# A hybrid of a two-way scan, convolution and attention: sums moved between engines, one image buffer halved, and a new set of due times

## Chip, cores and metric

The kernel runs on one core of a Trainium2 chip. The metric is the device time of one execution in microseconds; several executions are timed and their median is given. The core has five engines, each with its own instruction queue that is worked off in order: TensorE (PE, with its weight loads as PEld), VectorE (DVE), ScalarE (ACT), GpSimd (POOL) and SyncE (SP), which here only issues the transfers. All transfers of the main loop go through SP's one queue.

## The reference, cut

Eight images of 384 channels and 32 x 32 positions go through two layers.

```python
# layer 0, for each image
xn = rmsnorm(x)                                  # over channels
# mamba, forward and on the reversed tokens:
u, z   = split(xn @ in_proj.T)
u      = silu(conv1d(u))                         # 4 taps along tokens
dt, Bm, Cm = split(u @ x_proj.T)                 # 24, 16, 16
delta  = softplus(dt @ dt_proj.T + b)
h      = exp(delta * A) * h + (delta * u) * Bm   # 384 channels x 16 states, token by token
y      = sum_n(h * Cm) + u * D
y      = (y * silu(z)) @ out_proj.T
g      = (forward + backward) * scale_mod
local  = sigmoid(conv3x3(xn) + b) * xn
x      = x + res_scale * (g + local)
# layer 1, on tokens t (1024 x 384)
t = t + causal_attention(layernorm(t))
t = t + gelu(layernorm(t) @ kron(c_fc_1, c_fc_2).T) @ kron(c_proj_1, c_proj_2).T
```

The feed-forward's first weight is a Kronecker product of a 1536 x 32 and a 1 x 12 matrix. So layernorm(t) @ w_fc.T is a weighted sum over 12 neighbouring channels (weights c_fc_2, called c2 in the kernel), which leaves 32 numbers per token, followed by a product with c_fc_1.

## The kernel before

The kernel is in float32. It records all its instructions first, with a due time for each, and then a planner (`Plan`) puts them in order: it holds a cost for every instruction, lets each engine take the instruction that is ready by those costs and has the lowest rank (due time less a rush), gives out the buffers, and issues the whole list in that order. What runs on the chip is thus a fixed order on each queue, with semaphores in between. All instructions that are recorded so are put down to the helper's line L423, so the profile's groups are told apart by the names of tiles.

The time axis of the due times is counted in units of the scan. For each image there are four steps (`STEPS`): direction 1 on the second half of the tokens, direction 1 on the first half, direction 0 on the first, direction 0 on the second; a half has 512 tokens. In this text they are steps 0 to 3. Each step has 12 units (k = 0 to 11), so an image has 48. One unit of `scan` handles 64 channels with 8 of the 16 states, on 128 partitions (16 channels x 8 states) by 4 x 512:

- GpSimd multiplies du (delta times u, loaded as hs<-db) with B (br) in one instruction of 128 x 2048: hs<-hs,br.
- ScalarE makes four times exp(delta A) into PSUM (da<-dl,nega), in three buffers da.
- VectorE runs four scans along the tokens (hs<-da,hs).
- The product with C is one instruction of 128 x 2048. In units 2, 5, 8 and 10 (`POOL_C`; 1, 3, 6, 8 and 10 in the last image, `POOL_END`) it runs on GpSimd (hs<-hs,cr), in the others on VectorE (hs<-hs,cb).
- TensorE sums over the states into y (y<-hs,sel), which frees the buffer hs, of which there are five.

Everything else is spread over these units by due times. For an image b, `norm_in` (normalizing, the in-projection of u, and the store of the normalized image xn to the scratch xq, padded for the 3 x 3 convolution), `conv_tokens` and `prepare` (delta, B and C) run in the units of image b - 1 (`OTHERS`; image 0 has `FIRST`, image 1 `SECOND`). `local_branch` (the gate z, the 3 x 3 convolution and the local branch) runs at the end of the units of image b - 1. `project` (the out-projection, after steps 2 and 3), `attention` and `feed_forward` for each half (`LAYER1`) run from the last steps of the image itself into the units of the next one. Counted in units, the feed-forward of the first half falls into step 0 of the next image, that of the second half into step 2; the local branch falls into step 3 and the beginning of the next step 0.

Places that the change touches:

- xn (one buffer) holds a whole image of 3 x 32 x 33 per partition from `norm_in` until the second half's local branch has been computed.
- `local` loads x again into a tmp, multiplies the gate with xn and adds x, both on GpSimd (uc<-uc,xn and tmp<-tmp,uc), and stores the sum to the scratch lx.
- `project` loads lx as three tmp and lets TensorE transpose them into the same PSUM bank as the out-projection (w<-ident,tmp).
- `feed_forward` multiplies each normalized tile of tokens with c2 on GpSimd (xt<-xt,row_sb), sums 12 neighbours on VectorE (xr<-xt), and turns the sums with four matmuls of 32 columns per tile (w<-ident,xr).
- tmp has five buffers.

While nothing else is ready, the planner puts a matmul with zeros into y's open bank (y<-zero,ident), called a filler here.

Of the kernel before, what the change touches and what calls it, by code (L numbers as in the profile page):

```python
# [28 lines left out]
AX = mybir.AxisListType  # L29

P = 128
HB = 512
STEPS = [(1, 1), (1, 0), (0, 0), (0, 1)]
POOL_C = (2, 5, 8, 10)
POOL_END = (1, 3, 6, 8, 10)
TMP, SIDE = 5, 4
REPS = 4
RUSH = 3.54
START, LATER = -40.0, -8.0
LATER_US = 36.0  # L40


FIRST = (1, 3.32, 9.89, 13.26, 18.58, 22.35)
SECOND = (23.0, 0.55)
OTHERS = (4.41, 7.19, 11.9, 15.22, 22.12, 25.54, 30.53, 33, 41.81, 48.93)
BURST = 8.0
PROJECT = 1.79
LAYER1 = (39.24, 51.32, 61.95, 72.21, 83.03)
LAYER1_6 = (40.39, 50, 56.13, 65.96, 72.89)
LAYER1_7 = (37.95, 41.37, 46.15, 55.8, 61.15, 67.54, 71.0, 75.0, 81.0)  # L50
HASTE = 19.01
FREE = ["w", "da", "cb", "w", "da", "cb", "da"]
EXPS = 0.0
SCAN = (-1.34, -1.1, -0.6, -0.4, -0.33, 0.15, 0.75, 1.2)
class _Op:


# [19 lines left out]
class Plan:  # L77
# [8 lines left out]
    SWITCH = 1.3  # L86
    LOOSE = ("w", "tmp", "side")
    HURRY = 6.54
    PATIENCE = 1.92
    SETTLE = 0.2  # L90
    HOP = 0.18
    RATE = 300e3
    LAND = 2.54
    GATE = 3.413
    WARM, COLD = 0.8, 0.45
    KEEP = 0.65
# [330 lines left out]
def conv_attn_kernel(  # L427
# [21 lines left out]
    NB, C, H, W = x.shape  # L449
    L = H * W  # L450
    NC = C // P
# [3 lines left out]
    NJ = cp1T.shape[1]  # L455
    NI = C // NJ
    NF = cp1T.shape[0] // P
    NG = P // NJ
# [3 lines left out]
    NQ = 4  # L462
# [39 lines left out]
    def weight(shape, nm):  # L502
        return plan.tile(const, shape, nm)
# [199 lines left out]
        cp2.unsqueeze(1).to_broadcast([P, NJ, NI]),  # L703
    )
    emat = emat.rearrange("p j i -> p (j i)")
    plan.tile(ps_y, [P, HB], "y")
    plan.nothing = plan.slots["y"][0][:, :256], ident, zero.to_broadcast([P, 256])
    carry = weight([P, NU * SG, NQ], "carry")
# [5 lines left out]
    def tmp():  # L714
        return plan.tile(l0, [P, HB], "tmp", TMP)

    def load_x(b, h):
# [3 lines left out]
            plan.sync.dma_start(xt[cc], xv[b, :, cc, h * HB : (h + 1) * HB])  # L721
        return xt

    def xn_of(b, h):

        return xn_t[b][:, :, h * HR : (h + 1) * HR, :W]

    def norm_in(b, h):
        xt = load_x(b, h)
        yield  # L730
        if b not in xn_t:
            xn_t[b] = plan.tile(l0, [P, NC, H, WP], "xn")
        xn = xn_of(b, h)
# [13 lines left out]
        padded = xn_t[b][:, :, h * HR : (h + 1) * HR]  # L747
        plan.vector.memset(padded[:, :, :, W:], 0.0)
        at = 1 + (h * HR + 1) * WP
        for cc in range(NC):  # L750
            plan.sync.dma_start(
                xq[cc * P : (cc + 1) * P, at : at + HR * WP],
                padded[:, cc].rearrange("p r w -> p (r w)"),
            )
        yield
        for m in range(NC):
            pu = bank()
            for cc in range(NC):
                plan.tensor.matmul(
                    pu.rearrange("p (r w) -> p r w", w=W),  # L760
                    win[:, cc, m * P : (m + 1) * P], xn[:, cc],
                    start=cc == 0, stop=cc == NC - 1,
                )
            u = tmp()
            plan.scalar.copy(u, pu)
            plan.sync.dma_start(up[m * P : (m + 1) * P, UP + h * HB : UP + (h + 1) * HB], u)
            yield
# [31 lines left out]

    def local(b, h):  # L800

        cols = slice(h * HB, (h + 1) * HB)
        lx = lx_t[b, h] = plan.tile(dram, [C, HB], "lx", 4)
        sg = sg_t[b, h]
        sgf = sg.rearrange("p cc t -> p (cc t)")
        plan.scalar.activation(sgf, sgf, AF.Identity, bias=hrs, scale=hrs)
        for cc in range(NC):
            xt = tmp()
            plan.sync.dma_start(xt, xv[b, :, cc, cols])
            sgi = sg[:, cc].rearrange("p (r w) -> p r w", w=W)  # L810
            plan.gpsimd.tensor_mul(sgi, sgi, xn_of(b, h)[:, cc])
            plan.gpsimd.tensor_add(xt, xt, sg[:, cc])
            plan.sync.dma_start(lx[cc * P : (cc + 1) * P], xt)
            yield

    def gate(b, h):
# [131 lines left out]
    def scan(b, si, lo=0, hi=HB):  # L948
# [38 lines left out]
        for k in range(n_u):  # L987
# [93 lines left out]
    def project(b, h, t1, lo=0, hi=HB):  # L1081

        yz = [yz_t[b, h, lo, cc] for cc in range(NC)]
        lx = []
        for cc in range(NC):
            lx.append(tmp()[:, : hi - lo])
            plan.sync.dma_start(lx[cc], lx_t[b, h][cc * P : (cc + 1) * P, lo:hi])
        yield
        for i in range((hi - lo) // P):
            cols = slice(i * P, (i + 1) * P)  # L1090
            po = bank()
            for cc in range(NC):
# [4 lines left out]
            for cc in range(NC):  # L1097
# [22 lines left out]
    def normed(t1, ti0, nrm, i):  # L1120
        xt = plan.tile(l1, [P, C], "xt", 2)
        plan.scalar.activation(
            xt, t1[:, ti0 + i], AF.Identity,
            scale=nrm[:, 0, i : i + 1], bias=nrm[:, 1, i : i + 1],
        )
        return xt

    kv_t = {}

    def attention(b, t1, t0, n, end=False):  # L1130
# [7 lines left out]
        tile0, nt = t0 // P, n // P  # L1138
        nrm = token_norm(t1, tile0, nt)
        yield  # L1140
        if end:
            xT = plan.tile(l0, [P, NQ * HB], "hs", 5)[:, : NC * n]
            xT = xT.rearrange("p (cc t) -> p cc t", cc=NC)
        else:
            xT = plan.tile(l1, [P, NF // 2, HB], "gl")[:, :NC, :n]
        for i in range(nt):
            xt = normed(t1, tile0, nrm, i)
            pt = bank()
            for cc in range(NC):
                plan.tensor.transpose(  # L1150
                    pt[:, cc * P : (cc + 1) * P], xt[:, cc * P : (cc + 1) * P], ident
                )
            plan.scalar.copy(
                xT[:, :, i * P : (i + 1) * P],
                pt[:, :C].rearrange("p (cc t) -> p cc t", cc=NC),
            )
            yield

        cs = tmp()[:, :n]
# [87 lines left out]
    def feed_forward(b, t1, t0, n, direct=False):  # L1247
# [1 line left out]
        nrm = token_norm(t1, tile0, nt)  # L1249
        yield  # L1250

        xr = plan.tile(l1, [P, NT, NJ], "xr")
        for i in range(nt):
            xt = normed(t1, tile0, nrm, i).rearrange("p (j i) -> p j i", i=NI)
            plan.gpsimd.tensor_mul(xt, xt, c2.unsqueeze(1).to_broadcast([P, NJ, NI]))
            plan.vector.reduce_sum(xr[:, i], xt, axis=AX.X)
            yield
        px = bank()[:, :n]
        for i in range(nt):
            for g in range(NG):  # L1260
                plan.tensor.matmul(
                    px[g * NJ : (g + 1) * NJ, i * P : (i + 1) * P], xr[:, i], ident,
                    start=True, stop=True, skip_group_check=True,
                )
        xrT = plan.tile(l1, [P, HB], "q")[:, :n]
        plan.scalar.copy(xrT, px)
        yield
# [57 lines left out]
        plan.batch = None  # L1325

    def local_branch(b, h, a, e):
        plan.spread(gate(b, h), a, a + 0.4 * (e - a))
# [145 lines left out]
```

## Time and profile before

| | |
|---|---|
| Runs | 3231.9, 3232.3, 3235.58, 3239.41 us |
| Median of these | 3233.94 us |
| Profiled execution | 3253.27 us |
| Its span, first to last instruction | 3251.5 us |
| Mean granted clock of TensorE | 0.96 of full speed |
| DMA | 762.47 MB, mean 235 GB/s |
| Busy share of the DMA engines, early (120 to 400 us) | 0.93 to 0.94 |
| Busy share of the DMA engines, middle (400 to 790 us) | 0.82 |
| After the last scan (3133 to 3251.5 us) | 118.5 us: PE 108.5 busy, ACT 67.2, DVE 44.1, POOL 15.2 |

How to read what follows: a group's row gives the engine, the operation, output <- inputs by tile names, shapes and count, then busy time and the mean of one in ns, then the idle time of the engine just before these instructions and what ended it. A row of the stretches gives a piece of the span, its length, and the busy time of each engine in it. A row of the waits gives who waited for whom: total us, how often, and the longest. Matmuls in float32 appear as two rows in the trace for each one that is built, transposes as one.

### The profile page before, as it was taken

The page shows a single profiled execution, that of the slowest core. Times are in us where ns is not written, and L with a number is a line of the kernel's source. Part 1 is how long each engine was busy: PE and PEld are TensorE (multiplying, and loading weights), DVE is VectorE, ACT ScalarE, POOL GpSimd, SP SyncE. Part 2 cuts the span into 40 slices and gives each one's busy share as a digit, 9 for nine tenths or more (in the row PEclk, how much of TensorE's full clock was granted, in tenths as well). Part 3 has the DMA queues.
Part 4 walks back from the last instruction along what each step waited for, and adds up shares of the span by engine and source line. Part 5 has one row for each costly group of instructions (what it writes and reads, how often), then busy time and mean ns, then how long its engine had stood idle before and what let it go on. Part 6 is the DMA issues. An engine that isn't in the chain of part 4 may idle for free. (4 is left out here: it accounts for less than half of the span.)

```text
span 3251.5 us, 40064 instructions
## 1 busy us (share of the span) xinstructions
PE 2791.4 (86%) x11945; PEld 1189.7 (37%) x11945; DVE 2679.0 (82%) x2740; ACT 2216.5 (68%) x3609; POOL 2693.4 (83%) x923
## 2 busy tenths in 40 slices
PE   8887888988888888888789888898888888888789
PEld 3322333343333333343333433333333333333345
DVE  3688778797898798987999878988899879989972
ACT  3565566768676775868678676777767686677564
POOL 2888889788998889897898989888898878998950
PEclk8988999999999999999999999999999999899899
DMA  7999998778887797977978789787878779665520
GB/s 226 273 289 270 274 270 261 239 227 251 257 250 245 232 268 214 288 231 219 279 240 271 221 256 255 232 270 233 259 230 261 223 230 278 196 193 180 178 87 23
DMA packets 424462, 762.47 MB, mean 235 GB/s; under 512 B 51020, under 2 KB 70804, under 8 KB 424244
## 3 DMA queue, kind: packets, MB, share of 16 engines
q1 hardware_dynamic: 424116, 759.80, 77.7%
q8 instruction: 94, 1.54, 0.2%
q14 instruction: 124, 1.02, 0.1%
q0 software_dynamic: 128, 0.11, 0.0%
HBM read 617.92 MB, written 141.80 MB: 234 GB/s over the span
## 5 line engine op out<-in xcount | busy, mean ns | idle before, releaser
L423 POOL TENSOR_TENSOR hs<-hs,br 128x2048 f32<-128x2048 f32 (+1 forms) x395 | 1738.6, 4407 | 313.0 <-PE y L423 139.1
L423 ACT ACTIVATE da<-dl,nega 128x512 f32<-128x512 f32 (+1 forms) x1584 | 1055.6, 677 | 539.1 <-DVE hs L423 383.3
L423 DVE TENSOR_TENSOR_SCAN hs<-da,carry,hs 128x512 f32<-128x512 f32 (+1 forms) x816 | 938.9, 1202 | 150.4 <-ACT da L423 126.4
L423 DVE TENSOR_TENSOR_SCAN hs<-da,hs 128x512 f32<-128x512 f32 x768 | 883.5, 1202 | 147.4 <-ACT da L423 127.2
L423 POOL TENSOR_TENSOR hs<-hs,cr 128x2048 f32<-128x2048 f32 (+1 forms) x137 | 599.0, 4372 | 77.9 <-DVE hs L423 44.7
L423 DVE TENSOR_TENSOR hs<-hs,cb 128x2048 f32<-128x2048 f32 (+1 forms) x259 | 574.5, 2218 | 62.9 <-ACT carry L423 52.3
L423 PE MATMUL y<-hs,sel 128*32 128x512 f32 (+1 forms) x3168 | 481.4, 613 | 134.4 <-POOL hs L423 85.5
L423 PE MATMUL y<-zero,ident 128*128 128x256 f32 x1394 | 369.9, 397 | 0.0
L423 PEld LDWEIGHTS y<-zero,ident 128*128 128x128 f32 x1394 | 257.5, 196 | 147.7 <-issue 120.0
L423 PEld LDWEIGHTS y<-hs,sel 128*32 128x32 f32 x3168 | 89.9, 110 | 386.4 <-POOL hs L423 140.0
L421 ACT ACT_TABLE_LOAD x178 | 228.4, 1283 | 3.1
L423 PE MATMUL w<-q,fc1s 128*128 128x512 f32 (+1 forms) x388 | 195.3, 612 | 18.1 <-ACT gl L423 7.1
L423 PE MATMUL w<-v,p 128*128 128x384 f32 x546 | 197.2, 507 | 14.4 <-ACT p L423 12.9
L423 PE MATMUL w<-rep,cwt 128*32 128x512 f32 x744 | 180.0, 626 | 32.7 <-DMA rep<-up 27.1
L423 PE MATMUL w<-rep,cit 96*32 96x512 f32 x1152 | 176.8, 627 | 24.3 <-DMA rep<-xq 12.6
L423 PE MATMUL w<-wout,side 128*128 128x384 f32 x378 | 147.6, 521 | 36.7 <-DVE side L423 29.3
L423 ACT ACTIVATE uc<-w,vec 128x512 f32<-128x512 f32 x144 | 97.0, 679 | 92.5 <-PE w L423 76.1
L423 ACT COPY gl<-w 128x512 f32<-128x512 f32 (+2 forms) x254 | 136.9, 549 | 32.4 <-PE w L423 31.1
L423 PE MATMUL w<-xn,wz 128*128 128x512 f32 x288 | 138.1, 621 | 7.3 <-ACT uc L423 4.9
L423 PE MATMUL w<-xn,win 128*128 128x512 f32 x288 | 135.3, 611 | 4.7 <-ACT tmp L423 2.7
L423 PE MATMUL w<-wvs,gl 128*128 128x384 f32 x372 | 133.7, 501 | 5.5 <-ACT v L423 3.2
L423 PEld LDWEIGHTS w<-v,p 128*128 128x128 f32 x546 | 102.0, 195 | 99.3 <-ACT p L423 33.3
(204 smaller groups left out, 3201.6 us busy)
## 6 DMA issues: line engine op xcount, KB each, us to landing
dl<-dd SPq DMA_DIRECT2D x744, 256.0 KB, 5.7
hs<-db SPq DMA_DIRECT2D x744, 256.0 KB, 5.8
rep<-up SPq DMA_DIRECT2D x180, 257.5 KB, 6.1
rep<-xq SPq DMA_DIRECT2D x192, 222.4 KB, 6.3
tmp<-in_x_dram SPq DMA_DIRECT2D x96, 256.0 KB, 6.1
dd<-tmp SPq DMA_DIRECT2D x96, 256.0 KB, 4.6
db<-uc SPq DMA_DIRECT2D x96, 256.0 KB, 4.6
br<-bd SPq DMA_DIRECT2D x62, 256.0 KB, 4.8
```

Of the source, the lines that this page charges most:

```text
L421: self.nc.scalar.preload_act_table_set(table)
L423: op.call(*args, **{k: self._bind(v) for k, v in op.kw.items()})
```

## The change

- *Feed-forward's first sum.* The product with c2 on GpSimd, the sum on VectorE and the 16 small matmuls of a half are gone. Each tile of normalized tokens is transposed by TensorE (three transposes), evicted by ScalarE, and three matmuls with a matrix cmat (made once, c2 spread over channels and repeated for the four groups) give the sums for the half.
- *Adding x.* `local` no longer loads or adds x and stores the product with xn alone to lx. `project` loads three more tmp with x and transposes them into the same bank: six transposes per tile of 128 tokens in place of three.
- *The image by halves.* xn holds a half (3 x 16 x 33). `norm_in` stores it to xq as before; `local_branch` first loads the half back from xq (`load_xn`), due one unit before the branch.
- *tmp* has seven buffers in place of five.
- *Products with C.* In steps 0 and 2 five units (1, 4, 6, 8, 10) run them on GpSimd, in steps 1 and 3 four (2, 5, 8, 10), as before. The last image keeps its own set.
- *Due times and planner costs.* `FIRST`, `SECOND`, `OTHERS`, `LAYER1` and its variants, `SCAN`, `RUSH`, `HASTE`, and the planner's `PATIENCE`, `SETTLE`, `HOP` and `LAND` get other numbers, so that the whole order changes.

```diff
-POOL_C = (2, 5, 8, 10)
+POOL_C = ((1, 4, 6, 8, 10), (2, 5, 8, 10), (1, 4, 6, 8, 10), (2, 5, 8, 10))
-TMP, SIDE = 5, 4
+TMP, SIDE = 7, 4
-RUSH = 3.54
+RUSH = 2.75
-FIRST = (1, 3.32, 9.89, 13.26, 18.58, 22.35)
-SECOND = (23.0, 0.55)
-OTHERS = (4.41, 7.19, 11.9, 15.22, 22.12, 25.54, 30.53, 33, 41.81, 48.93)
+FIRST = (1, 3.88, 11.84, 15.58, 19.14, 21.28)
+SECOND = (21.3, 0.613)
+OTHERS = (4.45, 7.23, 12.19, 15.26, 22.16, 25.58, 30.33, 33.04, 41.85, 48.97)
-LAYER1 = (39.24, 51.32, 61.95, 72.21, 83.03)
+LAYER1 = (39.19, 52.83, 61.9, 73.47, 83.81)
-HASTE = 19.01
+HASTE = 27.94
-SCAN = (-1.34, -1.1, -0.6, -0.4, -0.33, 0.15, 0.75, 1.2)
+SCAN = (-1.34, -1.14, -0.48, -0.4, -0.33, 0.15, 0.75, 1.2)
...
-    PATIENCE = 1.92
-    SETTLE = 0.2
-    HOP = 0.18
+    PATIENCE = 1.86
+    SETTLE = 0.28
+    HOP = 0.0
-    LAND = 2.54
+    LAND = 2.73
...
+    def load_xn(b, h):
+        xn_t[b, h] = half_image()
+        for cc, rows in enumerate(rows_of(b, h)):
+            plan.sync.dma_start(xn_t[b, h][:, cc].rearrange("p r w -> p (r w)"), rows)
...
     def local(b, h):
...
         for cc in range(NC):
-            xt = tmp()
-            plan.sync.dma_start(xt, xv[b, :, cc, cols])
             sgi = sg[:, cc].rearrange("p (r w) -> p r w", w=W)
             plan.gpsimd.tensor_mul(sgi, sgi, xn_of(b, h)[:, cc])
-            plan.gpsimd.tensor_add(xt, xt, sg[:, cc])
-            plan.sync.dma_start(lx[cc * P : (cc + 1) * P], xt)
+            plan.sync.dma_start(lx[cc * P : (cc + 1) * P], sg[:, cc])
...
-            if k in (POOL_END if b == NB - 1 else POOL_C):
+            if k in (POOL_END if b == NB - 1 else POOL_C[si]):
...
     def project(b, h, t1, lo=0, hi=HB):
-        for cc in range(NC):
-            lx.append(tmp()[:, : hi - lo])
-            plan.sync.dma_start(lx[cc], lx_t[b, h][cc * P : (cc + 1) * P, lo:hi])
+        for src in (lx_t[b, h].rearrange("(cc p) t -> p cc t", p=P), xv[b, :, :, h * HB : (h + 1) * HB]):
+            for cc in range(NC):
+                lx.append(tmp()[:, : hi - lo])
+                plan.sync.dma_start(lx[-1], src[:, cc, lo:hi])
...
-            for cc in range(NC):
+            for k in range(2 * NC):
+                cc = k % NC
                 plan.tensor.matmul(
-                    po[:, cc * P : (cc + 1) * P], lx[cc][:, cols], ident,
-                    start=False, stop=cc == NC - 1, is_transpose=True, skip_group_check=True,
+                    po[:, cc * P : (cc + 1) * P], lx[k][:, cols], ident,
+                    start=False, stop=k == 2 * NC - 1, is_transpose=True, skip_group_check=True,
                 )
...
+    def turn_tile(xT, t1, ti0, nrm, i):
+        xt = normed(t1, ti0, nrm, i)
+        pt = bank()
+        for cc in range(NC):
+            plan.tensor.transpose(
+                pt[:, cc * P : (cc + 1) * P], xt[:, cc * P : (cc + 1) * P], ident
+            )
+        plan.scalar.copy(
+            xT[:, :, i * P : (i + 1) * P], pt[:, :C].rearrange("p (cc t) -> p cc t", cc=NC)
+        )
...
     def feed_forward(b, t1, t0, n, direct=False):
-        xr = plan.tile(l1, [P, NT, NJ], "xr")
+        xT = channels_down(n, direct)
         for i in range(nt):
-            xt = normed(t1, tile0, nrm, i).rearrange("p (j i) -> p j i", i=NI)
-            plan.gpsimd.tensor_mul(xt, xt, c2.unsqueeze(1).to_broadcast([P, NJ, NI]))
-            plan.vector.reduce_sum(xr[:, i], xt, axis=AX.X)
+            turn_tile(xT, t1, tile0, nrm, i)
             yield
         px = bank()[:, :n]
-        for i in range(nt):
-            for g in range(NG):
-                plan.tensor.matmul(
-                    px[g * NJ : (g + 1) * NJ, i * P : (i + 1) * P], xr[:, i], ident,
-                    start=True, stop=True, skip_group_check=True,
-                )
+        for cc in range(NC):
+            plan.tensor.matmul(px, cmat[:, cc], xT[:, cc], start=cc == 0, stop=cc == NC - 1)
```

More of the change, by code (lines that the diff above doesn't have):

```diff
@@ L33 @@
 STEPS = [(1, 1), (1, 0), (0, 0), (0, 1)]
-POOL_C = (2, 5, 8, 10)
+POOL_C = ((1, 4, 6, 8, 10), (2, 5, 8, 10), (1, 4, 6, 8, 10), (2, 5, 8, 10))
 POOL_END = (1, 3, 6, 8, 10)
-TMP, SIDE = 5, 4
+TMP, SIDE = 7, 4
 REPS = 4
-RUSH = 3.54
+RUSH = 2.75
 START, LATER = -40.0, -8.0
 LATER_US = 36.0
-FIRST = (1, 3.32, 9.89, 13.26, 18.58, 22.35)
-SECOND = (23.0, 0.55)
-OTHERS = (4.41, 7.19, 11.9, 15.22, 22.12, 25.54, 30.53, 33, 41.81, 48.93)
+FIRST = (1, 3.88, 11.84, 15.58, 19.14, 21.28)
+SECOND = (21.3, 0.613)
+OTHERS = (4.45, 7.23, 12.19, 15.26, 22.16, 25.58, 30.33, 33.04, 41.85, 48.97)
 BURST = 8.0
 PROJECT = 1.79
-LAYER1 = (39.24, 51.32, 61.95, 72.21, 83.03)
-LAYER1_6 = (40.39, 50, 56.13, 65.96, 72.89)
-LAYER1_7 = (37.95, 41.37, 46.15, 55.8, 61.15, 67.54, 71.0, 75.0, 81.0)
-HASTE = 19.01
+LAYER1 = (39.19, 52.83, 61.9, 73.47, 83.81)
+LAYER1_6 = (40.39, 50, 56.13, 65.94, 71.15)
+LAYER1_7 = (37.8, 41.37, 45.76, 55.34, 60.22, 66.54, 70.54, 75.9, 82.39)
+HASTE = 27.94
 FREE = ["w", "da", "cb", "w", "da", "cb", "da"]
 EXPS = 0.0
-SCAN = (-1.34, -1.1, -0.6, -0.4, -0.33, 0.15, 0.75, 1.2)
+SCAN = (-1.34, -1.14, -0.48, -0.4, -0.33, 0.15, 0.75, 1.2)
 class _Op:
@@ L705, in conv_attn_kernel @@
     emat = emat.rearrange("p j i -> p (j i)")
+    turn2 = plan.tile(l0, [P, HB], "tmp", TMP)[:, :C]
+    plan.vector.tensor_mul(
+        turn2.rearrange("p (j i) -> p j i", i=NI),
+        every.unsqueeze(2).to_broadcast([P, NJ, NI]),
+        c2.unsqueeze(1).to_broadcast([P, NJ, NI]),
+    )
+    pt = bank()
+    for cc in range(NC):
+        plan.tensor.transpose(
+            pt[:, cc * P : (cc + 1) * P], turn2[:, cc * P : (cc + 1) * P], ident
+        )
+    cmat = weight([P, NC, P], "cmat")
+    plan.scalar.copy(cmat.rearrange("p cc m -> p (cc m)"), pt[:, :C])
     plan.tile(ps_y, [P, HB], "y")
@@ L722, in load_x, with rows_of, half_image @@
         return xt
+    def rows_of(b, h):
+        at = 1 + (h * HR + 1) * WP
+        return [xq[cc * P : (cc + 1) * P, at : at + HR * WP] for cc in range(NC)]
+    def half_image():
+        return plan.tile(l0, [P, NC, HR, WP], "xn")
+    def load_xn(b, h):
+        xn_t[b, h] = half_image()
+        for cc, rows in enumerate(rows_of(b, h)):
+            plan.sync.dma_start(xn_t[b, h][:, cc].rearrange("p r w -> p (r w)"), rows)
     def xn_of(b, h):
-        return xn_t[b][:, :, h * HR : (h + 1) * HR, :W]
+        return xn_t[b, h][:, :, :, :W]
     def norm_in(b, h):
@@ L730, in norm_in @@
         yield
-        if b not in xn_t:
-            xn_t[b] = plan.tile(l0, [P, NC, H, WP], "xn")
-        xn = xn_of(b, h)
+        padded = half_image()
+        xn = padded[:, :, :, :W]
         ms = bank()
@@ L746, in norm_in @@
             )
-        padded = xn_t[b][:, :, h * HR : (h + 1) * HR]
         plan.vector.memset(padded[:, :, :, W:], 0.0)
-        at = 1 + (h * HR + 1) * WP
-        for cc in range(NC):
-            plan.sync.dma_start(
-                xq[cc * P : (cc + 1) * P, at : at + HR * WP],
-                padded[:, cc].rearrange("p r w -> p (r w)"),
-            )
+        for cc, rows in enumerate(rows_of(b, h)):
+            plan.sync.dma_start(rows, padded[:, cc].rearrange("p r w -> p (r w)"))
         yield
@@ L800, in local @@
     def local(b, h):
-        cols = slice(h * HB, (h + 1) * HB)
         lx = lx_t[b, h] = plan.tile(dram, [C, HB], "lx", 4)
@@ L1096, in project @@
                 )
-            for cc in range(NC):
+            for k in range(2 * NC):
+                cc = k % NC
                 plan.tensor.matmul(
-                    po[:, cc * P : (cc + 1) * P], lx[cc][:, cols], ident,
-                    start=False, stop=cc == NC - 1, is_transpose=True, skip_group_check=True,
+                    po[:, cc * P : (cc + 1) * P], lx[k][:, cols], ident,
+                    start=False, stop=k == 2 * NC - 1, is_transpose=True, skip_group_check=True,
                 )
@@ L1126, in normed, with channels_down @@
         return xt
+    def channels_down(n, end):
+        if end:
+            xT = plan.tile(l0, [P, NQ * HB], "hs", 5)[:, : NC * n]
+            return xT.rearrange("p (cc t) -> p cc t", cc=NC)
+        return plan.tile(l1, [P, NF // 2, HB], "gl")[:, :NC, :n]
+    def turn_tile(xT, t1, ti0, nrm, i):
+        xt = normed(t1, ti0, nrm, i)
+        pt = bank()
+        for cc in range(NC):
+            plan.tensor.transpose(
+                pt[:, cc * P : (cc + 1) * P], xt[:, cc * P : (cc + 1) * P], ident
+            )
+        plan.scalar.copy(
+            xT[:, :, i * P : (i + 1) * P], pt[:, :C].rearrange("p (cc t) -> p cc t", cc=NC)
+        )
     kv_t = {}
@@ L1140, in attention @@
         yield
[L1141 to L1145, printed above, removed]
-        for i in range(nt):
[L1147 to L1156, printed above, removed]
+        xT = channels_down(n, end)
+        for i in range(nt):
+            turn_tile(xT, t1, tile0, nrm, i)
             yield
@@ L1250, in feed_forward @@
         yield
-        xr = plan.tile(l1, [P, NT, NJ], "xr")
+        xT = channels_down(n, direct)
         for i in range(nt):
-            xt = normed(t1, tile0, nrm, i).rearrange("p (j i) -> p j i", i=NI)
-            plan.gpsimd.tensor_mul(xt, xt, c2.unsqueeze(1).to_broadcast([P, NJ, NI]))
-            plan.vector.reduce_sum(xr[:, i], xt, axis=AX.X)
+            turn_tile(xT, t1, tile0, nrm, i)
             yield
         px = bank()[:, :n]
-        for i in range(nt):
-            for g in range(NG):
-                plan.tensor.matmul(
-                    px[g * NJ : (g + 1) * NJ, i * P : (i + 1) * P], xr[:, i], ident,
-                    start=True, stop=True, skip_group_check=True,
-                )
+        for cc in range(NC):
+            plan.tensor.matmul(px, cmat[:, cc], xT[:, cc], start=cc == 0, stop=cc == NC - 1)
         xrT = plan.tile(l1, [P, HB], "q")[:, :n]
@@ L1327, in local_branch @@
     def local_branch(b, h, a, e):
+        plan.due = a - 1.0
+        load_xn(b, h)
         plan.spread(gate(b, h), a, a + 0.4 * (e - a))
```

## The prediction

> **What bounds the kernel now.** First the shares of the page:
>
> ```profile
> span 3251.5 us, 40064 instructions
> ...
> PE 2791.4 (86%) x11945; PEld 1189.7 (37%) x11945; DVE 2679.0 (82%) x2740; ACT 2216.5 (68%) x3609; POOL 2693.4 (83%) x923
> ```
>
> No engine is full; VectorE (DVE) and GpSimd (POOL) carry the same load, and TensorE's 2791 us hold 369.9 us of filler (y<-zero,ident, which only keeps the clock up). So I cut the span into scan steps: 32 of them, each with 12 products of du with B on GpSimd; the boundaries are where every twelfth of these products starts in GpSimd's timeline. The view of stretches for the four steps of image 2 (length; then busy time of PE, PEld, DVE, ACT, POOL; clock, DMA share, GB/s):
>
> ```profile
> 881.80:970.80 89.00, 78.79 (x323) 33.97 (x323) 85.01 (x93) 69.64 (x121) 83.65 (x30) 1.00 0.84 253
> 970.80:1067.10 96.30, 85.58 (x346) 37.84 (x346) 81.92 (x79) 66.25 (x108) 83.23 (x27) 1.00 0.80 247
> 1067.10:1171.90 104.80, 92.74 (x430) 36.86 (x430) 83.27 (x81) 80.16 (x123) 87.08 (x32) 1.00 0.74 236
> 1171.90:1262.20 90.30, 75.58 (x339) 29.51 (x339) 82.25 (x76) 57.11 (x87) 79.71 (x25) 0.91 0.91 257
> ```
>
> Means over images 1 to 6 of the same view: step 0 lasts 93.4 us (DVE 85.4, POOL 82.2), step 1 99.9 (85.2, 84.4), step 2 104.6 (82.6, 88.2, ACT 80.4), step 3 96.1 (87.3, 87.2). Steps 0 and 3 are short of idle: about 8 us are left to VectorE. Step 2 has 22 us of idle on VectorE and 16 on GpSimd, though it has no more work. The list of waits says what ends that idle time:
>
> ```profile
> ACT da L423 <- DVE hs L423: 383.3, 474, 5.6
> DVE hs L423 <- ACT da L423: 253.6, 107, 8.9
> ...
> POOL hs L423 <- PE y L423: 139.1, 46, 10.8
> ...
> POOL hs L423 <- DMA hs<-db: 84.3, 12, 30.9
> ```
>
> VectorE loses most to ScalarE's exponentials: few waits (107), up to 8.9 us, where ScalarE is in a block of other work. In image 2's step 2 they are 16.5 us, in its steps 0 and 3 0.3 and 1.0. GpSimd loses most to TensorE, whose y matmuls free the hs buffers.
>
> **The change, part by part.** The prices stand in the groups, kept apart by shape (busy and mean of one):
>
> ```profile
> L423 POOL TENSOR_TENSOR hs<-hs,cr 128x2048 f32<-128x2048 f32 x127 | 575.4, 4531 | 60.1 <-DVE hs L423 27.9 <-ACT carry L423 12.1 <-DVE sm L423 8.5
> ...
> L423 POOL TENSOR_TENSOR tmp<-tmp,uc 128x512 f32<-128x512 f32 x48 | 61.1, 1272 | 3.2
> ...
> L423 POOL TENSOR_TENSOR xt<-xt,row_sb 128x384 f32<-128x384 f32 x64 | 56.8, 912 | 7.7 <-ACT xt L423 7.7
> ```
>
> ```profile
> L423 DVE TENSOR_TENSOR hs<-hs,cb 128x2048 f32<-128x2048 f32 x245 | 557.6, 2276 | 62.6 <-ACT carry L423 52.3 <-ACT cb L423 5.7 <-ACT side L423 0.5
> ...
> L423 DVE TENSOR_REDUCE xr<-xt 128x32 f32<-128x384 f32 x64 | 33.3, 540 | 23.0 <-POOL xt L423 22.8
> ```
>
> GpSimd loses 48 additions of x (61.1 us) and 64 products with c2 (56.8), and takes 14 more products with C (two steps of seven images, 4.531 each: 63.4): 54.5 less. VectorE loses 64 sums (33.3) and 14 products (2.276 each: 31.9): 65.2 less. ScalarE takes 64 more evictions of a 128x384 bank (480 ns by the gl<-w row: 30.7) and, counted in the two built programs, has 162 table loads where it had 179 (17 by 1.283: 21.8 less): 8.9 more. Two of those loads per image fall away in step 2, where the softplus batch was cut in two.
>
> TensorE, by busy time per built instruction: 387 more transposes (0.185 for ident,tmp and 0.174 for ident,xt: 69 us), 48 matmuls with cmat (by the fc1s row, two passes, 187.1/180 = 1.04: 49), less 256 small ones with xr (25.3); and the new order holds 135 fewer fillers (369.9/697 = 0.53: 72 less). Real work grows by 93 us, 3.8% of the 2421 that are not filler.
>
> DMA: x's 48 pieces of 256 KB are loaded in project instead of in local, the stores to lx stay, and 48 loads xn<-xq of 264 KB are new: 13.0 MB on 762.5. On SP's queue the first three come right behind the in-projection and wait for TensorE's last readers of xn; the next three wait for GpSimd's last product of the half before.
>
> A rule speaks against the fifth product. The two engines' shares are 82% and 83% of one span, so they overlap for at least 65% of it; and the product on GpSimd takes 4518 ns in 75 to 260 us, where VectorE is 71 to 76% busy, and 4531 over the run. The Trainium skill (Perfetto Trace Analysis, Optimizing Scalar/DVE Operations) warns that GpSimd and VectorE share an SBUF read port, so that moving work between them might not help. By that rule 14 products would hold VectorE up for 63 us and take the whole gain; by the rows they hold up nothing. I go by the rows.
>
> Now step by step, since a gain counts only where the engine is needed. *Step 0* holds one feed-forward half, one local branch and a fifth product: VectorE 4 x 0.540 + 2.276 = 4.4 less; GpSimd 4 x 0.912 + 3 x 1.272 - 4.531 = 2.9 less. Both are near the limit; between -2.9 and -4.4 I take the middle, -3.7; in seven images -26. *Step 1* has nothing of it: 0. *Step 2*: VectorE 4.4 less, GpSimd 4.531 - 3.65 = 0.9 more, ScalarE 4 x 0.480 - 2 x 1.283 = 0.6 less; between +0.9 and -4.4 the middle, -1.8; in seven images -12. *Step 3*: GpSimd loses three additions (3.8), VectorE nothing; between 0 and -3.8 the middle, -1.9; in eight images -15. *Image 0* gets two fifth products (9.1) and loses six additions (7.6) while DMA is 92 to 98% busy: between +9 and -8, I take +2. *TensorE*: 3.8% on the 139 us for which GpSimd waits for it is +5; at worst a quarter of the 93 us reaches the scan (139 of GpSimd's 558 us of idle time are waits for TensorE), +23; at best, where the fillers that fall away make room, 0. *DMA*: image 0's six loads, 1.6 MB at 280 GB/s, are 5.6 if nothing hides them, 0 if all; I take +3, and in later steps the DMA engines are busy for 74 to 91%, which hides it. *The end* after the last scan (118.5 us in the stretches, GpSimd 15 and VectorE 44 busy) swaps GpSimd, VectorE and 16 small matmuls for three transposes and an eviction per tile: 0, within 5 either way. *The shifted dues* move instructions past each other on every queue; no row prices that. The nearest is the spread of like steps: step 0 takes 86.8 to 99.0 us in images 2 to 6 with the same work in it, so placing alone is worth 6 us either way in one step. If 1 us of it went one way in 28 steps, it would be 28 either way. I take 0.
>
> Sum: -26 - 12 - 15 + 2 + 5 + 3 = -43. The profiled execution took 3253.3 us (span 3251.5 and 1.8 around it), 0.6% over the median of 3233.9; it would take 3210, and the median 3191.
>
> If the larger share of transposes lowered the clock (0.96 over the run, 0.85 between 170 and 278 us), the matmuls would lengthen. The Trainium skill (TensorE: Matmul & The Clock Gate, Part 4) says that transposes do not count as TensorE being busy the way matmuls do. No row isolates that here; a fall of the clock by 3% makes 2.6 us of the 85.5 that TensorE is busy in a step, most of it beside other engines.
>
> **Rivals.** *A, the gain grows*: one softplus block instead of two lets the exponentials through, and a third of the 16.5 us wait in step 2 goes too (5.5 by seven images, 38). For it: the waits on ScalarE are few and long. Against: ScalarE has 9 us more to do in all. 3191 - 38 = 3153. *B, the gain is lost step by step*: each step keeps the end of its pair that is worst: step 0 -20, step 2 +6, step 3 0, image 0 +9, TensorE +5, DMA +5.6: +6, or 3240; no change by the bound below. For it: GpSimd is the fuller one in step 2. Against: in steps 0 and 3 VectorE is the fuller. *C, slower*: SP's queue. It works in order, and the three loads of the second half wait in it for GpSimd's last local product; project now takes six of seven tmp where it took three of five, and SP already waits 166.3 us for ScalarE to free tmp (longest 64.5). Behind stand hs<-db and dl<-dd, for which GpSimd waits 84.3 and ScalarE 134.3 us today. If GpSimd or tmp come late by the 7.5 us that its longest middle waits for TensorE show, in each of eight images, it is +60: 3191 + 60 = 3251. From 43/8 = 5.4 us per image it decides the sign. Against it: these loads stand far ahead of their use. *D*, that the edit does not do what it says, is out: the built orders hold the counts above.
>
> **How the numbers follow.** Forecast 0.50, A 0.22, B 0.12, C 0.16. The forecast's own range, from the step ends, TensorE, DMA and dues, is 3160 to 3222. To leave out no more than 2 in 10 the whole range takes in A's 3153 and a little beyond, and B, but only the edge of C: 3147 to 3242. About 0.2% (6.5 us) can be told from no change. Faster: forecast and A and a third of B, 0.76; within: half of B, 0.06; slower: C and the rest of B, 0.18.
>
> **What would show it.** GpSimd's busy time near 2639 and VectorE's near 2614; step 0 near 90, step 1 unchanged, step 2 near 103, step 3 near 94. A shows as step 2 near 97 with VectorE's wait for da falling below 200. C shows as SP's waits for GpSimd and tmp, and GpSimd's for hs<-db above 84. The forecast is wrong if step 1, which the edit leaves alone, moves by more than 3 us: then the dues decide, not the work.

## The result, and the profile after

The change makes the kernel slightly slower: 3241.81 us in the median of 46 runs against 3233.52 in 70 runs of before, ratio 1.0023 (95% interval 1.0014 to 1.0032; the two medians as they stand give 1.0026). The forecast was 3191. One of the 8 runs of b_both, an experiment below, took 6664.5 us, about twice the others, and stands outside its ratio. The profiled execution of after took 3238.8 us, close to its median; that of before took 3253.3, more than any of its 70 timed runs (up to 3252.8), so the two profiles must not be subtracted as they stand.

The shares of the page after:

```profile
span 3237.0 us, 39481 instructions
...
PE 2795.2 (86%) x11652; PEld 1179.5 (36%) x11652; DVE 2620.6 (81%) x2663; ACT 2219.1 (69%) x3657; POOL 2643.0 (82%) x825
```

The work fell as it was worked out: GpSimd by 50 us (forecast 54.5), VectorE by 58 (65); ScalarE rose by 3 (9) and TensorE, fillers included, by 4 (21). But the time did not follow. At the median, 3242 - 2643 = 599 us of GpSimd's time are idle, where before it was 3234 - 2693 = 541.

Two of the groups that were priced:

```profile
L423 POOL TENSOR_TENSOR hs<-hs,cr 128x2048 f32<-128x2048 f32 x141 | 639.3, 4534 | 89.7 <-DVE hs L423 54.8 <-ACT carry L423 34.2 <-DMA dl<-dd 0.8
```

```profile
L423 DVE TENSOR_TENSOR hs<-hs,cb 128x2048 f32<-128x2048 f32 x231 | 526.0, 2278 | 47.4 <-ACT carry L423 27.9 <-ACT cb L423 15.3
```

The prices hold (4534 and 2278 ns, before 4531 and 2276). What moved is the idle time in front of GpSimd's products with C: 60.1 us for 127 of them before, 89.7 for 141 now.

Image 2's four steps, in the columns used before and with the same rule for their boundaries (the start of every twelfth of GpSimd's products of du with B):

```profile
880.40:968.60 88.20, 80.25 (x291) 35.75 (x291) 80.71 (x93) 69.61 (x125) 80.46 (x23) 0.96 0.77 236
968.60:1068.80 100.20, 89.85 (x383) 39.31 (x382) 82.24 (x79) 71.56 (x114) 83.92 (x29) 1.00 0.86 255
1068.80:1169.70 100.90, 88.17 (x378) 33.42 (x376) 79.11 (x76) 78.48 (x125) 88.19 (x29) 1.00 0.87 254
1169.70:1256.30 86.60, 70.13 (x314) 29.53 (x314) 79.70 (x69) 51.63 (x79) 76.06 (x23) 0.92 0.96 268
```

Step 0 holds 4.3 us less of VectorE's work and 3.2 less of GpSimd's, close to the 4.4 and 2.9 worked out, and is 0.8 us shorter (88.2, before 89.0): VectorE is idle for 7.5 us where it was idle for 4.0. From the list of waits (who waited for whom: us, how often, longest):

```profile
ACT da L423 <- DVE hs L423: 333.3, 428, 5.2
DVE hs L423 <- ACT da L423: 261.4, 101, 10.9
...
ACT da L423 <- DMA dl<-dd: 169.8, 118, 5.8
...
POOL hs L423 <- PE y L423: 157.3, 59, 10.9
...
POOL hs L423 <- DVE hs L423: 95.0, 22, 12.6
```

Two of these rows in the profile before:

```profile
ACT da L423 <- DMA dl<-dd: 134.3, 104, 3.9
...
POOL hs L423 <- DVE hs L423: 54.6, 16, 10.6
```

ScalarE waits less for VectorE (383 before), but more for delta's loads (134 before); GpSimd waits more for TensorE (139 before) and for VectorE (54.6 before). No new wait stands out; several grew by 18 to 40 us, and orders of the same work differ by as much (GpSimd's wait for TensorE is 157, 202 and 176 us in the three orders of after's work below).

Stretches of single profiled executions, in us. They run from one of GpSimd's products of du with B to another, 48 to an image; the very first unit has its product on VectorE, so each stretch starts one unit late:

| Profile | ahead | image 0 | images 1 to 6 | image 7 | from the last product to the end |
|---|---|---|---|---|---|
| before | 73.1 | 398.6 | 2316.2 | 345.7 | 117.9 |
| before's work, neutral order (nb_rate below) | 71.9 | 397.0 | 2309.6 | 340.6 | 117.9 |
| before's work, after's due times (d_only below) | 68.4 | 413.5 | 2305.0 | 346.6 | 116.0 |
| after | 71.9 | 401.2 | 2294.7 | 348.2 | 121.0 |
| after's work, neutral order (na_rate below) | 73.8 | 405.3 | 2294.8 | 347.3 | 115.0 |
| after's work, another neutral order (na_rate2 below) | 73.6 | 401.1 | 2286.2 | 349.6 | 120.0 |

After and nb_rate have the same span (3237.0 us). After is 15 us shorter over images 1 to 6 and gives it back in image 0 (4), image 7 (8) and at the end (3). The other rows point the same way: images 1 to 6 take 2286 to 2295 us with after's work and 2305 to 2316 with before's, all the rest 941 to 944 and 927 to 945. So the work may pay some 3 us per image in the middle and lose part of it at both ends; with one profile of each order this is a hint, and no run tests it.

The last column is the stretch that was called "after the last scan" in the profile before (3133 to 3251.5 us). It starts with GpSimd's last product of du with B; VectorE's scans go on until 3169.2 us, 82.3 us from the end (after: 3155.5, 81.5 from the end).

### The profile page after: what moved, and what is told of

The parts are those of the page before. It is cut to its first block, busy times and chain, and to the rows that moved or that the text cites. A ratio compares the mean times of both kernels' runs of the same rounds, so it can differ in the third digit from the quotient of the medians.

```text
span 3237.0 us, 39481 instructions
## 1 busy us (share of the span) xinstructions
PE 2795.2 (86%) x11652; PEld 1179.5 (36%) x11652; DVE 2620.6 (81%) x2663; ACT 2219.1 (69%) x3657; POOL 2643.0 (82%) x825
## 5 line engine op out<-in xcount | busy, mean ns | idle before, releaser
L423 POOL TENSOR_TENSOR hs<-hs,cr 128x2048 f32<-128x2048 f32 (+1 forms) x151 | 662.9, 4390 | 124.8 <-DVE hs L423 84.5
L423 PE MATMUL y<-hs,sel 128*32 128x512 f32 (+1 forms) x3168 | 496.9, 617 | 162.2 <-POOL hs L423 111.0
L423 DVE TENSOR_TENSOR hs<-hs,cb 128x2048 f32<-128x2048 f32 (+1 forms) x245 | 543.0, 2217 | 49.6 <-ACT carry L423 29.8
L423 PE MATMUL y<-zero,ident 128*128 128x256 f32 x1124 | 302.2, 400 | 0.0
L423 PEld LDWEIGHTS y<-zero,ident 128*128 128x128 f32 x1124 | 206.8, 197 | 114.1 <-issue 90.7
L423 ACT COPY gl<-w 128x384 f32<-128x384 f32 (+2 forms) x316 | 166.7, 534 | 41.2 <-PE w L423 36.6
L423 PE MATMUL w<-rep,cwt 128*32 128x512 f32 x744 | 158.1, 624 | 22.4 <-DMA rep<-up 10.8
```

The source lines that it names most:

```text
L423: op.call(*args, **{k: self._bind(v) for k, v in op.kw.items()})
```

## The experiments

All ratios are against before, measured on the same chip. Where several edits are put together, S stands for the sums, the addition of x, the half image and tmp of after (the work), F for the fifth product with C, D for the due times and planner costs.

### Is it the work, the fifth product or the due times?

**s_only** (S), **f_only** (F), **d_only** (D) and **s_f** (S and F):

```diff
 # s_only: after, with the numbers of D as in before, and
-POOL_C = ((1, 4, 6, 8, 10), (2, 5, 8, 10), (1, 4, 6, 8, 10), (2, 5, 8, 10))
+POOL_C = ((2, 5, 8, 10),) * 4
 # f_only: before, and
-POOL_C = (2, 5, 8, 10)
+POOL_C = ((1, 4, 6, 8, 10), (2, 5, 8, 10), (1, 4, 6, 8, 10), (2, 5, 8, 10))
 # d_only: before, with the numbers of D as in after
 # s_f: after, with the numbers of D as in before
```

> The sums, the addition of x and the half image, with four products with C on GpSimd in every step and all due times and planner costs of before. The work theory (the work taken off GpSimd and VectorE shortens the steps, and the new due times lose it again): 0.98 to 0.99 of before. The order theory (what an engine saves becomes idle time, since the order in the queues sets the pace): 0.995 to 1.01. The cost theory (loading xn back, six tmp in project and more work on TensorE cost as much as is saved): above 1.005.

> Only the fifth product with C on GpSimd in steps 0 and 2. Work theory: 63 us go to GpSimd and 32 leave VectorE, a little slower, 1.000 to 1.010. Order theory: anything within 0.99 to 1.01, about as far from 1 as any other small edit. A theory that the fifth product is what ate the gain: 1.012 or more.

> Only the due times and planner costs of after, the work as before. Work theory: the new dues fit other work, so 1.010 to 1.020, enough to eat the 43 us forecast. Order theory: they are one more order, 0.99 to 1.01. If the new dues are better by themselves: below 0.995.

> All edits to the work (sums, x, half image, fifth product), with the due times and planner costs of before. Work theory: 0.980 to 0.990, the forecast gain without what the new dues lose. Order theory: 0.995 to 1.01. Cost theory: above 1.005.

**s_d** (S and D: after, with four products in every step) and **f_d** (F and D), which close the table:

> After, but with four products with C on GpSimd in every step. Order theory: one more order around dues that were not made for it, 1.008 to 1.016, slower than after although VectorE and GpSimd have the more even load on paper. Work theory: within 0.5% of after, 0.998 to 1.007.

> Before's work with the fifth product in two steps, and all dues of after. Order theory: 1.005 to 1.016. Work theory: above d_only (1.0056) by the fifth product alone, 1.006 to 1.015. It closes the table of all eight combinations: the mean of the four with the sums against the mean of the four without is the worth of the sums.

| | without S | with S |
|---|---|---|
| old dues, four products | 1 (before) | 1.0137 [1.0116, 1.0158] |
| old dues, F | 1.0142 [1.0119, 1.0165] | 1.0117 [1.0097, 1.0137] |
| D, four products | 1.0056 [1.0036, 1.0075] | 1.0143 [1.0116, 1.0169] |
| D, F | 1.0143 [1.0124, 1.0162] | 1.0023 [1.0014, 1.0032] (after) |

The work theory falls: s_f, with all the work of after, should have been at 0.98 to 0.99 and is at 1.0117. Over the four pairs S is worth +0.20% (mean of the right column less mean of the left), F +0.22% and D -0.08%, worked out from the table: nothing that helps. What stands out is that before and after each lie 1.2 to 1.4% below every neighbour in which S or F alone is changed; where the dues alone are changed, it is 0.56% (d_only against before) and 0.94% (s_f against after). Dues made for other work thus cost more than the work itself gives. Most of that loss lies in images 1 to 6, which take 2332 to 2344 us in the profiles of s_only, f_only, s_f, s_d and f_d (before 2316, after 2295), but in no one step: compared with before, the step that grew most, by some 3 us, is step 1 in s_only and s_d, step 0 in f_only and f_d, step 2 in s_f. Each is one profile.

By the expectations, s_only and s_f are beyond the order theory's 1.01 and where the cost theory put them, f_only is where the fifth product was to have eaten the gain, and d_only, s_d and f_d are where the order theory put them. The table itself speaks against the fifth product as the cause, since with the new dues it makes S faster (1.0143 to 1.0023); the costs are measured below. The granted clock doesn't sort the runs either: f_only (0.956), s_only (0.957) and f_d (0.958) have a lower mean than before in the same sessions (0.965 to 0.966), but s_d, as slow as f_d, has 0.964. Whether the lower clock is a cause or an effect of the slower order isn't shown.

The fifth product itself is not hampered by VectorE. f_only's group:

```profile
L423 POOL TENSOR_TENSOR hs<-hs,cr 128x2048 f32<-128x2048 f32 x141 | 639.2, 4533 | 81.0 <-ACT carry L423 33.7 <-DVE hs L423 26.2 <-DMA hs<-db 19.9
```

4533 ns for one, as before (4531).

### What is an order worth that nobody chose?

**nb_rate** and **na_rate** leave the work alone and change one number of the planner a little, which reorders all queues; **na_rate2** does it the other way.

```diff
 # nb_rate: before; na_rate: after
-    RATE = 300e3
+    RATE = 299e3
 # na_rate2: after
-    RATE = 300e3
+    RATE = 301e3
```

> Before, with nothing changed but one number of the planner, its assumed transfer rate, 299e3 in place of 300e3: the same work, another order. Order theory: slower by as much as the edits with old dues were, 1.005 to 1.015. Work theory: 0.998 to 1.003, since nothing of the work is changed.

> After, with the same neutral change, 299e3 in place of 300e3. Order theory: 1.005 to 1.015. If the edits are worth 1.3% once both kernels stand on an order that nobody chose: some 1.3% below nb_rate. If they are worth nothing: like nb_rate within 0.4%.

> After with another neutral change, the assumed transfer rate 301e3 in place of 300e3: a third order for the same work. Order theory: within 0.5% of after either way, 0.997 to 1.007. If the edits are better than their order here shows: below 0.997.

nb_rate: 1.0042 [1.0029, 1.0055]. na_rate: 1.0003 [0.9988, 1.0019]. na_rate2: 1.0039 [1.0023, 1.0055]. A neutral change of order is thus worth 0.2 to 0.4%, less than the 0.5 to 1.5% that the order theory had for the first two; na_rate is like nb_rate within 0.4%, as expected of edits that are worth nothing. Before's work in three orders (before, nb_rate, d_only) is at 1.0000, 1.0042, 1.0056, mean 1.0033; after's work in three (after, na_rate, na_rate2) at 1.0023, 1.0003, 1.0039, mean 1.0022. With three each, the two kinds of work can't be told apart, and the 0.23% by which after is slower is no larger than the spread between orders. (d_only is no neutral order, but one more order of before's work.)

### What does work taken off the two engines give, in the same order?

These kernels are planned like before (or after) and issued in exactly that order, but some marked instructions are cut to a few columns when they are issued. Their results then lack what was cut.

**b_both** cuts in before's order the 48 additions of x on GpSimd, the 64 sums of 12 channels on VectorE and 14 of VectorE's products with C. **b_pool** cuts GpSimd's 48 additions and 64 products with c2.

```diff
 # b_both and b_pool, in local
-            plan.gpsimd.tensor_add(xt, xt, sg[:, cc])
+            plan.gpsimd.tensor_add(xt[:, :16], xt[:, :16], sg[:, cc, :16])   # planned at full cost
 # b_both, in feed_forward
-            plan.vector.reduce_sum(xr[:, i], xt, axis=AX.X)
+            plan.vector.reduce_sum(xr[:, i, :1], xt[:, :1], axis=AX.X)
 # b_both, in scan, for k == 6, steps 0 and 2, images 0 to 6: the product with cb on 4 columns
 # b_pool, in feed_forward: the product with c2 on 12 columns
```

> Before's order, instruction by instruction, but the work that the change takes off is cut to a few columns: GpSimd's 48 additions of x, VectorE's 64 sums of 12 channels, and 14 of VectorE's products with C (unit 6 of steps 0 and 2 in images 0 to 6). Nothing is added for it. GpSimd has some 54 us less to do and VectorE some 57. Work theory (my prediction: 26 + 12 + 15 - 2 = 51 us before the costs): 0.980 to 0.988. Order theory (what an engine saves turns into idle time of that engine): 0.994 to 1.000.

> Before's order, with GpSimd's 48 additions of x and 64 products with c2 cut to a few columns: some 100 us of GpSimd's 2693, and nothing else. Work theory, if GpSimd is the bound: 0.970 to 0.980. If it is one of two: 0.985 to 0.992. Order theory: 0.995 to 1.000.

b_both: 0.9960 [0.9946, 0.9975]. b_pool: 0.9960 [0.9947, 0.9973]. Both are 13 us of 3234, and where the order theory put them. Page of b_both:

```profile
PE 2776.6 (86%) x11945; PEld 1183.4 (37%) x11945; DVE 2627.7 (82%) x2741; ACT 2212.7 (69%) x3609; POOL 2643.3 (82%) x923
```

GpSimd has 50 us less and VectorE 51, nearly what the change takes off, with none of its costs and in the order that suits before. 51 us were forecast for it, 13 came. This is what comes through in an order that is kept; what an order made for the lighter work could give is another question. In b_pool GpSimd has 94 us less. Two of its waits grew:

```profile
POOL hs L430 <- PE y L430: 164.0, 55, 10.1
...
POOL hs L430 <- DMA hs<-db: 102.0, 17, 30.0
```

In before they are 139.1 and 84.3: GpSimd is done earlier and waits longer for TensorE to free hs and for du to land. That is 43 of the some 80 us that did not come through; in b_both no wait of GpSimd tells it as plainly (144.7 for TensorE). Image 0 got shorter in both profiles (387 and 388 us, before 399, nb_rate 397), and images 1 to 6 a little (2300 and 2304 us, nb_rate 2310).

### What do the added parts cost?

**a_noload** and **a_pe**, in after's order: the loads of the half image cut to 8 numbers per row; and two of the three added transposes left out in project and in the feed-forward, whose eviction is cut to 16 columns.

```diff
 # a_noload, in load_xn
-            plan.sync.dma_start(xn_t[b, h][:, cc].rearrange("p r w -> p (r w)"), rows)
+            plan.sync.dma_start(xn_t[b, h][:, cc].rearrange("p r w -> p (r w)")[:, :8], rows[:, :8])
 # a_pe: in project, k = 3 and 4 are not issued; in the feed-forward's turn_tile, cc = 1 and 2 are not issued, and
-        plan.scalar.copy(xT[:, :, i * P : (i + 1) * P], pt[:, :C]...)
+        plan.scalar.copy(xT[:, :1, i * P : i * P + 16], pt[:, :16]...)
```

> After's order, with the loads of the half image cut to 8 numbers per row: the 48 transfers stand in the queue but move nothing. If the 13 MB and their place in SP's queue cost what the edits save: 0.985 to 0.995 of before. If they are hidden: 1.000 to 1.004, like after.

> After's order, without two of the three added transposes in project and in the feed-forward, and with the feed-forward's eviction cut to 16 columns: TensorE some 45 us less, ScalarE some 14. If the work that was moved to TensorE and ScalarE took the gain: 0.985 to 0.995 of before. If it lies under other work: 0.998 to 1.004.

a_noload: 1.0015 [1.0001, 1.0030], against after's 1.0023: the 13 MB cost 0.08%, not told apart from nothing. a_pe: 0.9999 [0.9983, 1.0014]: 0.24%, or 8 us, for 31 us less of TensorE and 19 less of ScalarE (45 and 14 were expected). Neither takes the gain: both lie where they were expected if the added parts are mostly hidden. The matmuls with cmat, the third transpose, and the place of the turned tokens in the one buffer gl, which the attention and the feed-forward's evictions also use, are taken apart by no run.

### Does any engine set the pace?

Four cuts in before's order, on one resource each, and one on three engines at once.

```diff
 # b_act, in feed_forward (halves that are not direct): evictions to gl and Gelu
-                        plan.scalar.copy(gl[:, k + i], ph[i])
+                        plan.scalar.copy(gl[:, k + i, :16], ph[i][:, :16])
-                plan.scalar.activation(gl, gl, AF.Gelu)
+                plan.scalar.activation(gl[:, :, :16], gl[:, :, :16], AF.Gelu)
 # b_pe, in conv: the matmuls with cit on one row of 32 positions in place of 16 rows
 # b_dma, in scan: dl loaded in half of its columns (the rest stays zero)
 # b_dve, in scan: for k in (7, 9) the product with cb on 4 columns
 # b_three: the cuts of b_pool, b_dve and b_act together
```

> Before's order; ScalarE's evictions and Gelu of the feed-forward cut to 16 columns: some 150 us of its 2216. If ScalarE's blocks hold up the exponentials and set the pace: 0.965 to 0.980 (half of it or more comes through). If no engine sets the pace alone (spread theory, a tenth to a fifth comes through, as for GpSimd): 0.990 to 0.996.

> Before's order; the 576 matmuls of the 3 x 3 convolution cut from 512 to 32 columns: some 100 to 160 us of TensorE's 2791. If TensorE's queue sets the pace: 0.965 to 0.980. Spread theory: 0.990 to 0.997.

> Before's order; the loads of delta cut to half their columns: the same transfers in the queue, some 100 MB less of 762. If the transfers set the pace: 0.94 to 0.975. Spread theory: 0.985 to 0.997.

> Before's order; VectorE's products with C of units 7 and 9 cut to 4 columns per row: some 130 us of its 2679. If VectorE sets the pace: 0.965 to 0.980. Spread theory: 0.990 to 0.996.

> Before's order with three cuts at once: GpSimd's as in b_pool, VectorE's as in b_dve, ScalarE's as in b_act, some 94, 125 and 143 us of busy time. If what comes through of each adds up: 0.40 + 0.28 + 0.99 = 1.7% less, 0.981 to 0.986. If the engines wait for each other in turn, so that cuts on all open what a cut on one leaves shut: below 0.975. If another thing (the transfers, TensorE) holds them all: above 0.988.

Cuts are the differences of busy time between the profile of before and that of the run; for the transfers, the queue's share of the 16 engines times the span (77.7% of 3251.5 less 68.6% of 3172.2). Time is the ratio's part of 3234 us. The pages of b_pool, b_dve, b_act, b_pe and b_three in this order, then the queue before and in b_dma:

```profile
PE 2781.6 (86%) x11945; PEld 1186.3 (37%) x11945; DVE 2678.0 (83%) x2740; ACT 2214.8 (69%) x3609; POOL 2599.6 (81%) x923
PE 2779.8 (86%) x11945; PEld 1188.0 (37%) x11945; DVE 2554.0 (79%) x2740; ACT 2212.5 (69%) x3609; POOL 2691.9 (84%) x923
PE 2762.7 (86%) x11945; PEld 1185.7 (37%) x11945; DVE 2681.6 (84%) x2741; ACT 2073.5 (65%) x3609; POOL 2692.4 (84%) x923
PE 2697.9 (83%) x11945; PEld 1177.3 (36%) x11945; DVE 2679.1 (83%) x2740; ACT 2216.0 (68%) x3609; POOL 2692.0 (83%) x923
PE 2760.5 (87%) x11945; PEld 1192.3 (38%) x11945; DVE 2557.2 (81%) x2741; ACT 2067.9 (65%) x3609; POOL 2597.8 (82%) x923
...
q1 hardware_dynamic: 424116, 759.80, 77.7%
...
q1 hardware_dynamic: 424116, 659.14, 68.6%
```

| Run | cut, us | ratio | time, us | comes through |
|---|---|---|---|---|
| b_pool | GpSimd 94 | 0.9960 [0.9947, 0.9973] | 13 | 14% |
| b_dve | VectorE 125 | 0.9972 [0.9955, 0.9988] | 9 | 7% |
| b_act | ScalarE 143 | 0.9901 [0.9878, 0.9923] | 32 | 22% |
| b_pe | TensorE 94 | 1.0015 [1.0000, 1.0030] | -5 | none |
| b_dma | transfers 350 (101 MB) | 0.9819 [0.9804, 0.9835] | 59 | 17% |
| b_three | 96 + 122 + 149 | 0.9834 [0.9814, 0.9855] | 54 | 15% |

No cut comes through by half. b_three is the sum of its parts (13 + 9 + 32 = 54, within its interval of 47 to 60): these cuts add up and do not open each other. Of the expectations, b_act's spread theory and b_three's sum were met; b_dve gave less than the spread theory had, b_pe nothing, and b_dma lies between its two ranges. The largest effects are not on VectorE and GpSimd, which the change relieves, but on ScalarE, which makes da, and on the transfers, which bring delta and du. In b_dma

```profile
ACT da L435 <- DVE hs L435: 388.4, 518, 5.2
...
DVE hs L435 <- ACT da L435: 208.1, 83, 9.9
...
ACT da L435 <- DMA dl<-dd: 54.8, 49, 4.2
```

ScalarE's wait for delta falls from 134 to 55 us, and VectorE's wait for da from 254 to 208. In b_act, whose cut is in the feed-forward and not in the exponentials, the latter falls as well:

```profile
DVE hs L431 <- ACT da L431: 217.8, 105, 10.0
```

b_pe is not a clean cut: with shorter matmuls TensorE was granted a lower clock (mean of its 12 runs 0.947, of before's 23 in the same session 0.965), so it leaves TensorE's part open.

## Why the prediction was wrong, step by step

- **The step that failed** is the sum "step by step": for each scan step I let the middle of what VectorE and GpSimd lose come through, 51 us in all before the costs. b_both measured nearly the same relief without costs at 13 us. I read "about 8 us are left to VectorE" in steps 0 and 3 as a sign that VectorE sets their length. It doesn't: 7% of b_dve's cut comes through, and image 2's step 0, with 4.3 us less of VectorE's work and 3.2 less of GpSimd's, got 0.8 us shorter. Over images 1 to 6 step 0, which was to give -26 of the 51, changed by -0.9 us a time (-1.6 against nb_rate, a neutral order of before's work) where -3.7 was forecast.
- **The work** was right: the counts hold, and the busy times of GpSimd and VectorE came out within 4 and 7 us. TensorE's work without fillers rose by 72 us (forecast 93).
- **The costs** were near: TensorE was +5, where a_pe shows 8 for a part of it together with ScalarE's evictions; the half image's loads were +3, where a_noload shows 3 and can't exclude 0. With 13 from b_both they leave some 2 us of gain: by this estimate, which adds up cuts in two orders, the edits as work are worth about nothing.
- **The dues** were taken as 0 with 28 either way. The size was about right and was what mattered: with the old work the new dues cost 0.56% (18 us), with the new work the old dues cost 0.94% more (1.0117 against 1.0023; 30 us). They are part of the edit and no separate term. The row that the bound was taken from was miscounted: in images 2 to 6 step 0 took 88.2 to 93.6 us, not 86.8 to 99.0.
- **My own test** said that the forecast is wrong if step 1 moves by more than 3 us. Two of the means that it starts from were miscounted. By the starts of every twelfth product, steps 0 to 3 of images 1 to 6 took 93.4, 97.8, 104.5 and 90.3 us in before (I had 99.9 for step 1 and 96.1 for step 3). Counted alike, after has 92.5, 99.1, 101.4 and 89.4, and nb_rate, with before's work, 94.1, 97.1, 104.7 and 89.1. Step 1 moved by 1.3 us, or 2.0 against nb_rate, and the forecast was wrong all the same. Step 2 gave more than forecast (-3.1, or -3.3 against nb_rate; forecast -1.8), step 3 less (-0.9, or +0.3; forecast -1.9).
- **The end** was taken as 0 within 5 either way. It came out at +3 (121.0 us against 117.9), though its stretch starts before the last scans.
- **Rival A** is out: VectorE's wait for da is 261 us, not below 200, and step 2 is at 101.4 us, not near 97. **Rival C** is not seen as described: GpSimd's wait for du fell from 84 to 57 us, though SP's wait for tmp rose from 166 to 200. **Rival B**, the gain lost step by step at 3240 us, hit the time, but by luck: it has step 2 growing by 0.9 us where it shrank by 3.1, and its mechanism, that the worse-off engine of each step decides, did not show, since relieving both engines gives little either.
- **The rule on the shared port** was rightly set aside: f_only's products take 4533 ns and its VectorE's products 2277, as before, though f_only is slower by 1.4%.
- **The clock** fell by a trace only: 0.963 in the mean of after's 46 runs, 0.965 to 0.967 in before's runs of the experiments' sessions (the profiled execution of before, with 0.960, is a low one). That is far from the 3% of the prediction's aside, and no run shows whether the transposes are the cause.

The Trainium skill (Perfetto Trace Analysis, Identifying the Most-Contended Engine) advises to take the engine with the highest occupancy and optimize that first, and says that for TensorE the share of time busy with matmuls is no good measure of how near the kernel is to its limit. Here the runs differ from the first half: VectorE (82%) and GpSimd (83%) let 7 and 14% of a cut through, ScalarE (68%) 22%.

Open is where exactly dues that were made for other work lose their 0.6 to 1.4%, and what TensorE's work alone is worth. No version that does the whole work was measurably faster than before.

## What to carry to other kernels

Where several engines are each at 80 to 86% and wait for one another in turn, as here, a shorter instruction can mostly become a longer wait: cut the instruction to nothing in the unchanged order and measure what comes through before building the change that saves it. Where a planner or a hand has set the order, compare a change of work with neutral reorderings of both kernels, since the order alone moves the time by as much as the edit. And base a sum of steps on a profile that lies at the median of the runs, with the steps of every profile counted by one rule.

## What was not expected of the hardware

A us cut from ScalarE's feed-forward work (ScalarE 68% busy) was worth more than a us cut from VectorE's products with C (82% busy): 22% of the cut comes through, against 7%. Cutting 576 matmuls from 592 to 196 ns (median of one of the two passes) took 94 us off TensorE, came with a lower granted clock (0.947 in the mean of the runs, before 0.965) and gained nothing.
